# Both ends of a self-attention stage: feature loads cut into quarters, the first keys rotated earlier, softmax scalings moved to ScalarE, transposed-weight moves moved from ScalarE's queue to GpSimd's

## The chip, the cores and the metric

The program runs on one core of a Trainium2 chip. The metric is the device time of one execution in microseconds (us). The execution before the change takes 3047.43 us, the median of three runs (3047.22 to 3047.49). A difference of less than about 0.2% (6 us) can't be told from no change.

## The reference, cut to what matters

One post-norm decoder layer, in float32, over 2048 tokens of width 512:

```
x = layernorm(x + self_attention(x))        # 32 heads of 128, 8 key/value heads, no mask
x = layernorm(x + cross_attention(x, ctx))  # 32 sequences of 64 tokens
x = layernorm(x + ffn(x))

# self-attention; k_sel, v_sel are 512 gathered cache rows, 64 new tokens are appended
q, k, v = x @ wq.T, x @ wk.T, x @ wv.T      # q and k rotated by cos, sin
k_full, v_full = concat(k_sel, k[0]), concat(v_sel, v[0])     # 576 keys
out = softmax(q k_full^T / sqrt(128)) v_full @ wo.T
```

Every query attends to the same 576 keys (512 cached, 64 new). The change touches self-attention alone, at its first few and its last four units of work.

## The kernel before, in words

**Units.** Self-attention is 128 units, `units[n] = (g, tb, h)`: 8 groups g of 4 heads, 4 token blocks tb of 512 tokens, 4 heads h of the group. The four units of one (g, tb) are called a block here, b = n // 4; there are 32 blocks. A unit has four tiles i of 128 queries.

**A tile** (`scores(n, i)`): TensorE (PE) writes 128x576 scores to one of two PSUM buffers `s` (L651). VectorE (DVE) takes the row maximum `nmax` (L656), ScalarE (ACT) computes the exponentials `p` and their sum `den` (L659), DVE takes the reciprocal (L668), scales `p` by it (L669) and transposes 32x32 blocks of `p` into `T` (L677; in the order of instructions, the transpose of a tile stands behind the maximum of the next tile, except for a unit's last tile).

**Moves.** When `T` of a unit is full, `move(n)` (L689) issues 16 DMAs of 64 or 80 KB, SBUF to SBUF, which finish the transpose into `pT`. They are issued by SyncE's queue (SP). For the units in `short` (0, 1, 2, 124, 125, 126) only 12 of the 16 go there; the last four (`ranges = (3,)`) are issued one unit later by ACT's queue (`move(n - 1, (3,), nc.scalar)`).

**Values.** Two units later, `values(n - 2)` and `shared_values` multiply `pT` with the gathered values (L697, tile `po`), and ACT copies the result to `oT` (L720).

**Between the tiles**, PE works on two other matrix products, each in seven steps of 8 matmul instructions (L312, a Strassen-Winograd scheme with sums of operands): the queries of the next block (`q_step`; PSUM tiles `q_..`) and the output projection of an earlier one (`w_step`; `w_..`). The sums of their operands are made by GpSimd (POOL): `token_sums` (`tx1` to `tx4`), `left_sums` (weights), `output_sums` (`so1` to `so4`), 1.27 us each. In the first unit the products are what is left of block 0's queries (`last_products`: 3, 7 and 4); in the last four units there are no queries left, so only two or so products a unit stand between the tiles.

**Loads.** `load_features` fetches 512 tokens of `xT` (1 MB) with one DMA at the end of a block, ahead of that unit's moves in SP's queue; block 2's is issued at unit 0. At unit 124 the same is done for the first encoder block `encT` (1 MB), and at the end of unit 123 the eight DMAs of cross-attention's first weights (`load_kv_left`, tile `xwkv`) are put ahead of that unit's moves.

**Queues and order.** The instruction order of PE, DVE and ACT is the one written by hand; SP's and POOL's order, behind the start, is chosen when the program is built. A DMA waits, before it is issued, for the DMA that stood eight places earlier in the count of all hardware-queue DMAs (SP's and ACT's together); POOL's DMAs have a count of their own, of eight as well. An instruction that waits holds what stands behind it on its engine.

**Start.** Before unit 0, keys of group 0 are gathered by POOL (`gather_keys`, four indirect DMAs, tile `kn`), rotated in two halves by DVE and POOL (`rotate`, L593 to L598, into `kr`), transposed by PE (L632, `startbank`), and copied to `kT` by ACT (L635). Meanwhile PE makes four of block 0's seven query products.

Of the kernel before, what the change touches and what calls it, by code (L numbers as in the profile page):

```python
# [9 lines left out]
F32 = mybir.dt.float32  # L10
I32 = mybir.dt.int32
AF = mybir.ActivationFunctionType
ALU = mybir.AluOpType
# [3 lines left out]
P = 128  # L17
DIM = 512
NH, NKV, HD = 32, 8, 128
REP = NH // NKV  # L20
NT = 2048
SEQ = 64
TB = 512
NTB = NT // TB
# [28 lines left out]
def decoder_layer(  # L53
# [52 lines left out]
    def token_room(b, name):  # L106
        return act.tile([P, NC, TB], F32, tag=f"xT{b % 2}", name=name)

    def load_features(dst, src, tb, queue=nc.sync):
        queue.dma_start(  # L110
            out=dst, in_=src[:, tb * TB : (tb + 1) * TB].rearrange("(c p) n -> p c n", p=P)
        )

    def rows(src, tb):
        return src[tb * TB : (tb + 1) * TB, :].rearrange("(p j) f -> p j f", p=P)
# [100 lines left out]
    def left_sums(eng, a11, a12, a21, a22, s):  # L216
        eng.tensor_tensor(s[3], a11, a21, ALU.subtract)
        eng.tensor_tensor(s[1], a21, a22, ALU.add)
        eng.tensor_tensor(s[2], s[1], a11, ALU.subtract)
        eng.tensor_tensor(s[4], a12, s[2], ALU.subtract)  # L220
# [245 lines left out]
              for g in range(NKV)]  # L466
    KV_ORDER = (1, 6, 5, 7, 2, 4, 3)

    def load_kv_left(gp, pre):

        w = operands(pre, f"xwkv{gp}")
        s21 = w[5]
        for dst, (k, m) in ((w[1], (0, 0)), (w[2], (1, 0)), (w[4], (1, 1)), (s21, (0, 1))):
            for i in range(2):
                c0 = (i * NKV + 2 * gp + m) * HD
                nc.sync.dma_start(
                    out=dst[:, :, i * HD : (i + 1) * HD],
                    in_=xwkv[k * HF : (k + 1) * HF, c0 : c0 + HD].rearrange(
                        "(c p) n -> p c n", p=P
                    ),  # L480
                )
        left_sums(nc.gpsimd, w[1], w[2], s21, w[4], {1: w[5], 2: w[6], 3: w[7], 4: w[3]})
        return w

    def keys_values(gp, tb, tiles, tags):
# [14 lines left out]
    with ExitStack() as ph:  # L500
# [143 lines left out]
        def scores(n, i):  # L644


            g, tb, h = units[n]
            u = f"{g}_{tb}_{h}_{i}"
            s = sc.tile([P, 2, 512], F32, tag="sc", name=f"s{u}")
            for a in range(2):  # L650
                nc.tensor.matmul(  # L651
                    s[:, a, :HALF], qTs[n // REP][:, units[n][2], i * P : (i + 1) * P],
                    kTs[g][:, a * HALF : (a + 1) * HALF], start=True, stop=True,
                )
            nmax = small.tile([P, 1], F32, tag="nmax", name=f"nmax{u}")
            nc.vector.tensor_reduce(nmax, s[:, :, :HALF], AX.XY, ALU.max, negate=True)  # L656
            p = sb.tile([P, NKEY], F32, tag="p", name=f"p{u}", bufs=4)
            den = small.tile([P, 1], F32, tag="den", name=f"den{u}")
            nc.scalar.activation(  # L659
                p.rearrange("q (a k) -> q a k", a=2), s[:, :, :HALF], AF.Exp,  # L660
                bias=nmax, accum_out=den,
            )
            if i == 0:
                Ts[n] = sb.tile([P, NBK, TPB, SQ], F32, tag="T", name=f"T{g}_{tb}_{h}")
                flush()
            else:
                turn(n, i - 1)
            nc.vector.reciprocal(den, den)  # L668
            nc.vector.tensor_scalar(p, p, den, None, ALU.mult)  # L669
            ps_[n, i] = p  # L670
            if i == TPB - 1:
                turn(n, i)
# [132 lines left out]
        nc.vector.tensor_tensor(wq0[5], wq0[5], wq0[4], ALU.add)  # L805
        nc.vector.tensor_tensor(t[2], q[1, 1], t[1], sub)
        nc.vector.tensor_tensor(wq0[6], wq0[5], wq0[1], sub)
        nc.vector.tensor_tensor(wq0[3], wq0[2], wq0[6], sub)
        nc.vector.tensor_tensor(nrm2, cs2, cs2, ALU.mult)
        nc.vector.tensor_tensor(sn2, sn2, sn2, ALU.mult)  # L810
        nc.vector.tensor_tensor(nrm2, nrm2, sn2, ALU.add)
# [10 lines left out]
        z = first.mul("z", 5, True)  # L822
        y = first.mul("y", 6, True)
        new_keys(0)
        rotate(0, 0, NKT // 2)
        nc.vector.tensor_tensor(c[1, 1], z, c[1, 0], ALU.add)
        nc.vector.tensor_tensor(c[0, 1], y, c[1, 0], ALU.add)
        rotate(0, NKT // 2, NKT)
        for j in range(NKT):
            gather_values(0, j)  # L830
        cached_keys(0, "s0")
        nc.vector.tensor_tensor(t[3], q[1, 1], q[0, 1], sub)
        nc.vector.tensor_tensor(t[4], q[1, 0], t[2], sub)
        tok[1] = token_sums(xTs[1], "tx1", nc.gpsimd)
        wo_cur[0] = load_right(woT[columns(0), :], "wo0", nc.gpsimd, first=wo_cur[0])

        def last_products(i):
            if i == 3:
                first.mul("z", 3)
                reads.append(lambda: nc.vector.tensor_tensor(c[0, 1], z, c[0, 1], ALU.add))  # L840
            elif i == 7:
                first.mul("y", 7)
                reads.append(lambda: nc.vector.tensor_tensor(c[1, 1], y, c[1, 1], ALU.add))
            else:
                first.mul("y", 4)
                reads.append(lambda: nc.vector.tensor_tensor(c[1, 0], y, c[1, 0], ALU.add))
# [15 lines left out]
        for n in range(N):  # L862
            b, h = divmod(n, REP)
            g, r = units[n][0], n % PER
            if r == REP and g + 1 < NKV:
                load_group(g + 1)
            if r in gathers and g + 1 < NKV:
                gather_keys(g + 1, gathers[r])
            if 0 < n <= PER:


                b2, j = divmod(n - 1, TPB)
                nc.scalar.dma_start(out=acc[b2][:, j, :], in_=rows(x, b2)[:, j, :])
            if r == 2 * REP and g + 1 < NKV:
                later.append(lambda g=g: new_keys(g + 1))
            if r == 2 * REP + 1 and g + 1 < NKV:
                rotate(g + 1)
                later.append(lambda g=g: cached_keys(g + 1))
            if n == N - REP:
                encT[0] = big.tile([P, NC, TB], F32, tag="qT", name="encT0", bufs=2)  # L880
                load_features(encT[0], encT_in, 0)
            steps = {0: "qwqw", 1: "qw q", 2: "wqwq", 3: "w qw"}[h]

            def step(place):
                if n < REP:

                    i = {(0, 0): 3, (0, 1): 7, (0, 3): 4}.get((n, place))
                    if i:
                        last_products(i)
                    elif (n, place) in ((0, 2), (1, 0), (1, 1), (1, 2), (1, 3), (2, 0), (2, 2)):  # L890
                        q_step(n)
                elif steps[place] == "q":
                    q_step(n)
                elif steps[place] == "w":
                    w_step(b - 2 if h < 2 else b - 1)
                flush()

            def spare_bank():

                if n % 2 == 0 and later:  # L900
                    later.pop(0)()

            scores(n, 0)
            step(0)
            spare_bank()
            scores(n, 1)
            if n - 1 in short:
                move(n - 1, (3,), nc.scalar)
            if n >= 2:
                values(n - 2, 0, 2 if n % 2 == 0 else 3)  # L910
            step(1)
            scores(n, 2)
            step(2)
            if r in gathers and g + 1 < NKV:
                gather_values(g + 1, gathers[r])
            scores(n, 3)
            if n >= 2:
                values(n - 2, 2 if n % 2 == 0 else 3, NKT)
                if n % 2:
                    shared_values(n - 2)  # L920
            step(3)
            spare_bank()
            if h == REP - 1:
                if b + 2 < NB:
                    g2, tb2, _ = units[(b + 2) * REP]
                    if tb2 == 0:
                        wq_cur[g2] = load_left(wqT[:, columns(g2)], f"wq{g2}", nc.gpsimd)
                    tok[b + 2] = token_sums(xTs.pop(b + 2), f"tx{g2}_{tb2}", nc.gpsimd)
                elif b + 2 == NB:
                    kvw[0] = load_kv_left(0, "wq")  # L930
                else:
                    encR[0] = token_sums(encT[0], "te0", nc.gpsimd)
            if h == REP - 1 and b + 3 < NB or n == 0:

                b2 = b + 3 if n else 2
                xTs[b2] = token_room(b2, f"xT{b2}")
                load_features(xTs[b2], xT_in, b2 % NTB)
            move(n, (0, 1, 2) if n in short else range(NQD))

        encT[1] = big.tile([P, NC, TB], F32, tag="qT", name="encT1", bufs=2)
        load_features(encT[1], encT_in, 1)
        room = sb.tile([P, NBK, TPB, SQ], F32, tag="T", name="kvroom")
        room = room.rearrange("p b t k -> p (b t k)")
        tiles = [
# [504 lines left out]
```

## Time and profile before

| | |
|---|---|
| median of three runs | 3047.43 us |
| the profiled execution, its own time | 3049.76 us |
| its span in the profile | 3048.0 us |
| granted TensorE clock, mean | 0.997 |
| busy: PE / DVE / ACT / POOL | 3014.4 / 2200.1 / 783.8 / 946.9 us |
| self-attention, roughly | 18 to 1840 us of the span |
| idle PE, whole span (span less busy) | 33.6 us |

A row of the timeline starts with the start and the length in us of a run of like instructions; `x8` is their number, and the bracket at the end gives the idle time of the engine before the first of them and what ended it. PE executes matmuls one behind another and their ends are modelled, so a row of PE that is longer than others of the same kind and count also hides a loss. `SPq`, `ACTq` are DMAs issued by SP's and ACT's queue. Stretches can be asked for one by one, with the granted clock of each.

### The profile page before, as it was taken

How to read it: one execution, taken by the hardware profiler on the slowest of the kernel's cores; microseconds unless marked ns; L12 is line 12 of the kernel's file. 1: busy time of each engine (PE TensorE's matmuls, PEld its weight loads, DVE VectorE, ACT ScalarE, POOL GpSimd, SP SyncE). 2: the span in 40 equal slices, each digit the busy share in tenths (PEclk: the TensorE clock that was granted, in tenths of full speed). 3: DMA queues.
4: the chain of work that ended last, by engine and by line, in shares of the span. 5: the costliest groups of instructions: out<-in, count | busy, mean ns of one | idle time of the engine just before them, and what ended most of it. 6: DMA issues, size and time to landing. Idle time of an engine off the chain costs nothing.

```text
span 3048.0 us, 42453 instructions
## 1 busy us (share of the span) xinstructions
PE 3014.4 (99%) x14848; PEld 2321.9 (76%) x14848; DVE 2200.1 (72%) x4069; ACT 783.8 (26%) x1892; POOL 946.9 (31%) x774
## 2 busy tenths in 40 slices
PE   8999999999999999999999999999999999999998
PEld 6677777777777777777777768998888888888875
DVE  7777787777777777777877763546666666666787
ACT  2323223223222222222332221111111111111233
POOL 4231321321321321321321223035544444444420
PEclk9999999999999999999999999999999999999999
DMA  5444444444444444444444354351121121121121
GB/s 171 129 130 129 110 115 126 109 113 126 108 114 129 105 121 124 108 123 119 106 126 108 87 133 141 115 160 56 49 63 56 49 65 55 50 67 52 52 61 42
DMA packets 214931, 304.97 MB, mean 100 GB/s; under 512 B 45888, under 2 KB 108864, under 8 KB 214720
## 3 DMA queue, kind: packets, MB, share of 16 engines
q1 hardware_dynamic: 200048, 286.90, 34.7%
q10 hardware_dynamic: 12624, 11.16, 1.3%
q0 software_dynamic: 2048, 4.20, 0.5%
q8 instruction: 120, 1.97, 0.3%
q14 instruction: 91, 0.75, 0.1%
HBM read 107.05 MB, written 20.97 MB: 42 GB/s over the span
## 4 chain that ended last, share of the span: by engine, by line
PE 94%; DVE 2%; SPq 1%; DMA 1%; issue 1%; ACT 1%; POOL 0%; ACTq 0%; DVEq 0%; POOLq 0%
PE po L697 16%; PE s L651 15%; PE sx L1091 2%; PE pox L1163 2%; PE w_2y L312 1%; PE q_3y L312 1%; PE w_0y L312 1%; PE w_3y L312 1%; PE q_2y L312 1%; PE qx_0y L312 1%; PE wx_0y L312 1%; PE wx_3y L312 1%; PE qx_2y L312 1%; PE qx_1y L312 1%; PE wx_1y L312 1%; PE w_1y L312 1%
## 5 line engine op out<-in xcount | busy, mean ns | idle before, releaser
L659 ACT ACTIVATE p<-s,nmax 128x576 f32<-128x576 f32 x512 | 379.1, 740 | 1250.0 <-DVE nmax L656 1233.2
L651 PE MATMUL s<-kT,qT 128*128 128x288 f32 x2048 | 578.0, 408 | 4.9 <-ACT p L659 4.2
L697 PE MATMUL po<-pT,v 128*128 128x512 f32 (+1 forms) x1280 | 552.7, 605 | 6.2 <-DMA pT<-T 4.5
L651 PEld LDWEIGHTS s<-kT,qT 128*128 128x128 f32 x2048 | 388.4, 191 | 108.2 <-issue 19.7
L656 DVE TENSOR_REDUCE nmax<-s 128x1 f32<-128x576 f32 x512 | 384.0, 750 | 62.9 <-PE s L651 62.9
L677 DVE STREAM_TRANSPOSE T<-p 128x576 f32<-128x576 f32 x512 | 394.1, 770 | 4.4
L697 PEld LDWEIGHTS po<-pT,v 128*128 128x128 f32 (+1 forms) x1280 | 214.4, 190 | 208.5 <-issue 182.3
L669 DVE TENSOR_SCALAR p<-p,den 128x576 f32<-128x576 f32 x512 | 316.1, 617 | 17.9
L668 DVE RECIPROCAL den<-den 128x1 f32<-128x1 f32 x512 | 83.9, 164 | 230.9 <-ACT p L659 221.3
L283 POOL TENSOR_TENSOR so<-oT,oT 128x512 f32<-128x512 f32 x32 | 40.7, 1272 | 551.2 <-ACT oT L720 533.9
L286 POOL TENSOR_TENSOR so<-oT 128x512 f32<-128x512 f32 x32 | 40.6, 1270 | 351.2 <-ACT oT L720 100.6
L283 POOL TENSOR_TENSOR sox<-oTx,oTx 128x512 f32<-128x512 f32 x32 | 40.5, 1266 | 296.8 <-ACT oTx L1182 216.0
L1182 ACT ACTIVATE oTx<-pox,bv 128x128 f32<-128x128 f32 x256 | 73.7, 486 | 117.6 <-PE pox L1163 117.6
L224 POOL TENSOR_TENSOR tx<-xT 128x512 f32<-128x512 f32 x31 | 39.6, 1278 | 206.2 <-PE q_3z L312 65.0
L659 ACT ACTIVATION_READ_ACCUMULATOR p<-s,nmax 128x1 f32 x512 | 98.7, 193 | 0.0
L1292 POOL TENSOR_TENSOR txx<-x1T 128x512 f32<-128x512 f32 x31 | 39.3, 1268 | 174.6 <-PE qx_3z L312 75.2
L1108 ACT ACTIVATE ex<-ex 128x512 f32<-128x512 f32 x64 | 40.4, 631 | 201.7 <-DVE ex L1107 201.7
L1184 DVE TENSOR_SCALAR oTx<-pox,bv 128x128 f32<-128x128 f32 x256 | 72.6, 422 | 8.5 <-PE pox L1163 8.5
L1091 PEld LDWEIGHTS sx<-kvx,qTx 128*64 128x64 f32 x2048 | 62.3, 138 | 10.6 <-issue 10.6
L720 ACT COPY oT<-po 128x512 f32<-128x512 f32 x128 | 68.3, 587 | 4.7 <-PE po L697 3.8
L1091 PE MATMUL sx<-kvx,qTx 128*64 128x64 f32 x2048 | 66.7, 224 | 0.0
L1163 PE MATMUL pox<-pTx,kvx 64*128 64x256 f32 x512 | 64.6, 389 | 0.7 <-DMA pTx<-Tx 0.7
(443 smaller groups left out, 5746.1 us busy)
## 6 DMA issues: line engine op xcount, KB each, us to landing
pT<-T SPq DMA_DIRECT2D x1016, 80.0 KB
pT<-T SPq DMA_DIRECT2D x1008, 64.0 KB
xT<-in_xT SPq DMA_DIRECT2D x31, 1024.0 KB
kvx<-kv SPq DMA_DIRECT2D x32, 512.0 KB
pTx<-Tx SPq DMA_DIRECT2D x256, 64.0 KB
kv<-c SPq DMA_DIRECT2D x30, 512.0 KB
wo<-in_woT SPq DMA_DIRECT2D x32, 256.0 KB
xwq<-in_xwq SPq DMA_DIRECT2D x32, 256.0 KB
```

The costliest lines, as they stand in the source:

```text
L283: nc.gpsimd.tensor_tensor(t[1], a[1, 0], a[1, 1], ALU.add)
L312: nc.tensor.matmul(self.banks[b][:, m, :], self.left[i][:, k, m * P : (m + 1) * P], self.right[i][:, k, :], start=(first and m + k == 0), ...
L651: nc.tensor.matmul(s[:, a, :HALF], qTs[n // REP][:, units[n][2], i * P : (i + 1) * P], kTs[g][:, a * HALF : (a + 1) * HALF], start=True, s ...
L656: nc.vector.tensor_reduce(nmax, s[:, :, :HALF], AX.XY, ALU.max, negate=True)
L659: nc.scalar.activation(p.rearrange("q (a k) -> q a k", a=2), s[:, :, :HALF], AF.Exp, bias=nmax, accum_out=den,)
L668: nc.vector.reciprocal(den, den)
L669: nc.vector.tensor_scalar(p, p, den, None, ALU.mult)
L677: nc.vector.transpose(Ts[n][:, :, i, :], ps_.pop((n, i)).rearrange("q (b k) -> q b k", k=SQ))
L697: nc.tensor.matmul(pos[n].rearrange("d (a q) -> d a q", a=NQD), vs[units[n][0]][rows, v, :], pTs[n // 2][rows, :, chunk, :], skip_group_ch ...
L1091: nc.tensor.matmul(s[b * SEQ : (b + 1) * SEQ, i * REP + h, :], qTs[n][:, h, pr * HF + c0 : pr * HF + c0 + SEQ], kvs[n][:, pr, 0, c0 : c0 + ...
L1163: nc.tensor.matmul(po[pr, b][:, i, :].rearrange("d (h a j) -> d h a j", h=REP, a=2), kvs[n][r, pr, 1, i * HD : (i + 1) * HD], pTs[n][r, :, ...
L1182: nc.scalar.activation(dst, src, AF.Identity, bias=bias)
```

## The change

- `load_pieces` loads a feature block in four DMAs of 256 KB (one of the four groups of 128 features each). The pieces of block b + 2 are issued two by two in the first and second unit of block b (second and third unit for b = 0), in place of one 1 MB load at the end of block b - 1. The first encoder block's four pieces are spread over units 124 to 127 and the eight weight loads `xwkv` over units 124 to 126 (three, three, two), each ahead of the moves of its unit; the second encoder block comes in four pieces as well.
- The two halves of `rotate(0, ...)` come earlier in DVE's order, among the sums of the first weights, and product 3 of block 0's queries is put ahead of the first scores. One product less follows the fourth tile of unit 0 or 1.
- In units 0 to 3 all tiles, and in units 124 to 127 the tiles 1 and 3, are scaled by ACT (`activation(p, p, AF.Copy, scale=den)`) and not by DVE.
- The four moves of the `short` units that ACT's queue issued are issued by POOL's.

```diff
+    def load_pieces(dst, src, tb, *cs):
+        for c in cs:
+            nc.sync.dma_start(
+                out=dst[:, c, :], in_=src[c * P : (c + 1) * P, tb * TB : (tb + 1) * TB]
+            )
...
-    def load_kv_left(gp, pre):
+    def kv_left_parts(gp, pre):
...
-                nc.sync.dma_start(
+                loads.append(lambda dst=dst, k=k, i=i, c0=c0: nc.sync.dma_start(
...
+        return w, loads, lambda: left_sums(
+            nc.gpsimd, w[1], w[2], s21, w[4], {1: w[5], 2: w[6], 3: w[7], 4: w[3]}
+        )
...
             nc.vector.reciprocal(den, den)
-            nc.vector.tensor_scalar(p, p, den, None, ALU.mult)
+            if n < REP or n >= N - REP and i % 2:
+                nc.scalar.activation(p, p, AF.Copy, scale=den)
+            else:
+                nc.vector.tensor_scalar(p, p, den, None, ALU.mult)
...
         nc.vector.tensor_tensor(wq0[6], wq0[5], wq0[1], sub)
+        rotate(0, 0, NKT // 2)
         nc.vector.tensor_tensor(wq0[3], wq0[2], wq0[6], sub)
+        rotate(0, NKT // 2, NKT)
...
         new_keys(0)
-        rotate(0, 0, NKT // 2)
         nc.vector.tensor_tensor(c[1, 1], z, c[1, 0], ALU.add)
         nc.vector.tensor_tensor(c[0, 1], y, c[1, 0], ALU.add)
-        rotate(0, NKT // 2, NKT)
+        nc.vector.tensor_tensor(t[3], q[1, 1], q[0, 1], sub)
         for j in range(NKT):
             gather_values(0, j)
         cached_keys(0, "s0")
-        nc.vector.tensor_tensor(t[3], q[1, 1], q[0, 1], sub)
+        first.mul("z", 3)
         nc.vector.tensor_tensor(t[4], q[1, 0], t[2], sub)
+        nc.vector.tensor_tensor(c[0, 1], z, c[0, 1], ALU.add)
...
-            if n == N - REP:
-                encT[0] = big.tile([P, NC, TB], F32, tag="qT", name="encT0", bufs=2)
-                load_features(encT[0], encT_in, 0)
+            b2, k = b + 2, h - (b == 0)
+            if b2 < NB and k in (0, 1):
+                if k == 0:
+                    xTs[b2] = token_room(b2, f"xT{b2}")
+                load_pieces(xTs[b2], xT_in, b2 % NTB, 2 * k, 2 * k + 1)
+            if n >= N - REP:
+                if n == N - REP:
+                    encT[0] = big.tile([P, NC, TB], F32, tag="qT", name="encT0", bufs=2)
+                    kvw[0], kv_loads, kv_sums = kv_left_parts(0, "wq")
+                load_pieces(encT[0], encT_in, 0, h)
+                for load in kv_loads[3 * h : 3 * h + 3]:
+                    load()
+                if n == N - 2:
+                    kv_sums()
...
-                    i = {(0, 0): 3, (0, 1): 7, (0, 3): 4}.get((n, place))
+                    i = {(0, 0): 7, (0, 2): 4}.get((n, place))
                     if i:
                         last_products(i)
-                    elif (n, place) in ((0, 2), (1, 0), (1, 1), (1, 2), (1, 3), (2, 0), (2, 2)):
+                    elif (n, place) in ((0, 1), (0, 3), (1, 0), (1, 1), (1, 2), (2, 0), (2, 2)):
                         q_step(n)
...
             if n - 1 in short:
-                move(n - 1, (3,), nc.scalar)
+                move(n - 1, (3,), nc.gpsimd)
...
-                elif b + 2 == NB:
-                    kvw[0] = load_kv_left(0, "wq")
-                else:
+                elif b + 2 > NB:
                     encR[0] = token_sums(encT[0], "te0", nc.gpsimd)
-            if h == REP - 1 and b + 3 < NB or n == 0:
-                b2 = b + 3 if n else 2
-                xTs[b2] = token_room(b2, f"xT{b2}")
-                load_features(xTs[b2], xT_in, b2 % NTB)
             move(n, (0, 1, 2) if n in short else range(NQD))
...
         encT[1] = big.tile([P, NC, TB], F32, tag="qT", name="encT1", bufs=2)
-        load_features(encT[1], encT_in, 1)
+        load_pieces(encT[1], encT_in, 1, *range(NC))
```

## The prediction

> **What bounds the kernel now.** I read the page's busy table first, then PE's waits, then PE's timeline at both ends of self-attention, and last the queues and engines named there. PE is busy for 3014.4 of 3048.0 us, so little can be had, and all of it lies where PE waits or runs slowly. From 200 to 1760 us PE's waits sum to 1.3 us; the change's places are the first four and the last four units. There PE's timeline reads:
>
> ```profile
> 45.33 1.88 PE L697 MATMUL po<-pT,v 128*128 128x512 f32 x4
> 47.85 1.24 PE L651 MATMUL s<-kT,qT 128*128 128x288 f32 x4 [0.64 <-ACT p L659]
> ...
> 55.55 1.24 PE L651 MATMUL s<-kT,qT 128*128 128x288 f32 x4 [1.81 <-ACT p L659]
> 58.49 2.29 PE L651 MATMUL s<-kT,qT 128*128 128x288 f32 x4 [1.70 <-ACT p L659]
> 60.58 4.46 PE L697 MATMUL po<-pT,v 128*128 128x512 f32 x6
> ...
> 1776.74 2.81 PE L697 MATMUL po<-pT,v 128*128 128x512 f32 x6 [1.20 <-issue]
> ...
> 1792.12 3.75 PE L697 MATMUL po<-pT,v 128*128 128x512 f32 x4 [3.11 <-DMA pT<-T]
> ```
>
> See the brackets, and then the lengths: four score matmuls take 1.24 us at 55.55 and 2.29 behind the next gap; four `po` take 1.88 at 45.33 and 3.75 behind the gap at 1792. The stretches say why, in the column behind the busy times (granted clock):
>
> ```profile
> 58.00:62.00 4.00, 3.50 (x6) 2.19 (x7) 2.67 (x7) 1.27 (x4) 0.00 (x0) 0.50 0.38 110
> 66.00:80.00 14.00, 14.00 (x53) 9.05 (x52) 11.69 (x23) 6.60 (x15) 3.26 (x3) 1.00 0.61 166
> 1794.00:1798.00 4.00, 4.00 (x8) 2.29 (x7) 0.86 (x3) 0.04 (x1) 0.00 (x0) 0.50 0.73 185
> ```
>
> So both ends pay the gap and about 4 us at half clock after it. What the gaps wait for is on ACT and SP:
>
> ```profile
> 53.32 1.24 ACTq L689 DMA_DIRECT2D pT<-T  x2
> 54.67 0.74 ACT L659 ACTIVATE p<-s,nmax 128x576 f32<-128x576 f32 x1 [3.94 <-DVE T L677]
> ```
> ```profile
> 44.60 0.37 SPq L110 DMA_DIRECT2D xT<-in_xT  x1
> 45.65 44.88 SPq L689 DMA_DIRECT2D pT<-T  x53
> ```
> ```profile
> 1760.31 4.47 SPq L476 DMA_DIRECT2D xwkv<-in_xwkv  x8
> 1764.88 10.02 SPq L689 DMA_DIRECT2D pT<-T  x16
> 1775.01 0.52 SPq L110 DMA_DIRECT2D encT<-in_encT  x1
> 1775.88 35.94 SPq L689 DMA_DIRECT2D pT<-T  x36
> ```
>
> ACT's exponentials stand behind its own queue's moves, which wait for the DMA eight places earlier; at 45.65 that is held up by the 1 MB load issued at 44.60 (the chain of waits has "45.65 7.65 DMA pT<-T"). At the end, 8 weight loads and 1 MB stand in front of the moves that PE waits for at 1792. The third limit is the serial loop of a tile, in the chain of waits:
>
> ```profile
> 39.53 0.68 DVE nmax L656
> ...
> 40.29 0.84 ACT p L659 x2
> ...
> 41.15 0.17 DVE den L668
> ...
> 41.35 0.52 DVE p L669
> 41.87 0.60 DVE qT L364
> 42.47 0.68 DVE nmax L656
> ```
>
> It turns once in 2.94 us; PE's tile with one product is 0.97 + 1.73 = 2.70 (chain rows "PE s L651 x4", "PE q_2x L312 x8").
>
> **The change, part by part: the start.** From the end of the key transposes (18.93) to unit 4's first scores (68.83) 49.9 us pass. PE's work in it, at full clock: 16 scores x 0.97 = 15.5, 10 products x 1.73 = 17.3, `po` 3.44 + 2.57 + 1.92 = 7.9; sum 40.7. So 9.2 us are lost. None of this work is removed; only its order and the waits change.
> - Product 3 ahead of the first scores: it fills the 0.75 us that the first scores waited for ACT's key copy. Its DVE read (0.6) delays the first maximum, within the 1.5 us DVE was idle before it. The rotation moved up (eight DVE operations, about 2.2 us; POOL's four with it) doesn't start PE earlier: the transposes at 18.26 follow 17.30 + 1.0 us of PE work without a gap. 0 to 1.0 us, taken at 0.75.
> - ACT's scaling has no row. Nearest is ACT's exponential of 128x512 in SBUF in cross-attention (631 ns), scaled by size 0.7 us; from above the row of `p` itself, 0.74. In the loop it runs beside DVE's next maximum (0.68), so the loop falls from 2.94 to 0.17 + 0.6 + 0.68 + 0.84 + 0.1 = 2.4, below PE's 2.70; in unit 3 without products 1.8 against PE's 2.1. At a unit's last tile it costs 0.2 more than DVE's 0.52, since the transpose waits for it. DVE's own rows stretched by POOL (1.32 at 25.67, 1.58 at 50.96 for L669) go as well. ACT holds 0.84 + 0.7 + at most 0.6 of copies per tile: under 2.7.
> - The four moves leave ACT, so the 3.94 us wait goes. On POOL no direct DMA has a row; nearest are the gathers of as many 512-byte rows:
>
> ```profile
> L559 POOL DMA_INDIRECT v<-in_v_cache,row x32: 940/944/1483, 18.3 to 1483.5; - x32
> ...
> DMA to landing us min/median/max: 2.5/2.9/5.7
> ```
>
>   With 0.3 us between issues (73.79 after 72.53) a move costs POOL 1.25 us, four 5.0, and lands 2.9 later (from above 6.6, the median of the `kn` gathers; below, SP's 2.0). What queues behind them: POOL's `wo` sums end at about 35.7 (five us earlier sums follow PE's earlier products), unit 0's four run to 40.7 and land by 43.6; PE needs them at 44.2. `tx_2` sums behind them are due from 66. Unit 1's run 44.8 to 49.8, landed 52.7, due 53.3; unit 2's 54 to 59, due 63.
> - The load of block 2 in quarters and block 3's 1 MB out of unit 0's end: SP's first move of unit 1 goes at 44.1 with nothing large in front. Twelve at 0.64 (16 in 10.02) end at 51.8 and land 2.0 later, 53.8, against 53.3: 0.5 us of wait stays.
>
> Walking PE, DVE and ACT through units 0 to 3 with these rows leaves about 0.6 us of loop at unit 3, 0.5 of moves and 0.3 of boundaries: 9.2 - 1.4 = 7.8 us won.
>
> **The end.** From 1773.43 (scores of unit 125) to 1814.23 (values of unit 126) 40.8 us pass; the same rows sum to 32.7, so 8.1 are lost. Now unit 123's 16 moves go first, at 1762.6, and land by 1775 (wait of 1.20 gone). One encoder quarter and three weights (0.5 each) follow, and unit 124's twelve moves run 1775 to 1782.7, landed 1784.7; PE gets to them at 1787.2: the 3.11 and the slow clock behind it go. POOL issues unit 125's four between three `so` sums: 4 x 1.25 + 3 x 1.35 = 9.1 from 1786.4, last one landed 1797.2, due 1798.5; `so2` is ready at 1791.6, due 1795.8. The `xwkv` and `te` sums end at about 1811, due 1815. Half the scalings stay on DVE: there the loop is still 2.3, and two accumulations (0.6, 1.21) stand in it, so 1.5 us remain at units 126 and 127, and 0.5 for unit 126's moves. 8.1 - 2.0 = 6.1 us won.
>
> **The middle.** 31 blocks get three DMAs more each on SP (1.5 us of 0.5 each) beside 64 moves x 0.64 = 41 us in a block of 56: hidden; the load is due a whole block later than its issue. POOL's `so2`, `so4` now stand ahead of `tx3`, which is 2.6 us later, with `tx1` after it as before: hidden. Two or three waits on `pT` and `wq` (0.64 at 197.78, 0.44 and 0.20 near 633 to 651) may shrink: 0.5.
>
> **Two rules of the Trainium skill against the trace.** "DMA: Bandwidth & Descriptors", section "Bandwidth", "Measured", says to batch DMAs to 1 MiB and more, since each has about 2.0 us fixed. By it, four quarters (2.6 each) take 10.4 us in place of 4.4; at the end, with two encoder blocks in quarters, 12 us would be against us. The trace: SP issues move behind move every 0.64 us while each takes 2 to land, so the fixed part overlaps; only 0.5 us of SP each counts, and there is room for it. I take the trace. "TensorE: Matmul & The Clock Gate", section "Part 1: The HAM clock gate", has the clock halve after an idle window of about 3.4 us. By it gaps of 1.81 and 1.70 with a burst between cost only themselves, and the start would give 2.0 us less (1.12 + 0.41 + 0.46 over the full-clock lengths). The rows above show half clock, so I count them; the same rows warn that a gap left at two or three us costs twice.
>
> **Sum.** 7.8 + 6.1 + 0.5 = 14.4 us. The span 3048.0 becomes 3033.6; the profiled execution's 3049.76 becomes 3035.4. That one is 2.3 above the median of the runs, so the median becomes 3047.4 - 14.4 = 3033.0. If all is won at both ends and in the middle: 9.2 + 8.1 + 1.3 = 18.6, 3029.
>
> **Rivals.**
> - *POOL's moves come late* (6.6 us to land): unit 0's wait 2 us, unit 125's 3, each with half clock behind it (2 to 3 us): some 7.5 us given back, 3040.5. For it: `kn`'s 6.6. Against: `v` gathers in the same stage, 2.9.
> - *SP stays the bound of the start*: 53 moves in 44.88 us is 0.85 each; at that pace unit 1's land at 56.3, 3 us late, and the clock drops: 5.5 back, 3038.5. Against: the 0.85 holds the wait for the 1 MB load.
> - *Slower: a direct move costs POOL far more than a gather.* It has a row per block of `T`, 128 or 160 runs. POOL is in order, so each us over the 1.6 that fits unit 0's and 1's slack is paid four times at five places, and beyond 2.3 us each the gaps pass 3 us and add 3 of slow clock. At 2.3 the gain is gone; at 3.0 it is 5 x (5.6 + 3) - 14.4 = 29 worse, and halving that for overlap, 3060. Against: the gathers' 0.94, never over 1.48.
> - *The waits go but PE waits as long later* (unit 5's moves on a full SP queue, or the accumulations before cross-attention): 3046.
>
> **How the numbers follow.** Both ends won 0.72; POOL late 0.11, SP bound 0.09, slower 0.06, nothing 0.02. The likeliest gives 3033.0, with its own bounds 3029 to 3037. The range 3028.5 to 3041.5 takes in the SP case and most of POOL's. A measurement can tell 0.2% (6.1 us) from no change; so faster is below 3041.3: 0.72 + 0.08 + 0.06 = 0.86; same 0.08; slower 0.06.
>
> **What would show it.** Right: no PE gap over 1 us and clock 1.0 from 19 to 1850; unit 4's scores near 61 and values of unit 126 near 1800 (8 and 6 earlier, together); ACT never behind a DMA; POOL's moves near 1.25 us apart. Wrong: `po` waiting for `pT` near 44, 53 or 1790 with half clock after it, or POOL's moves over 2 us apart.

## The result, and the profile after

The changed kernel takes 3037.33 us (median of nine runs, 3034.30 to 3041.03); the kernel before beside it took 3047.33 (nine, 3045.55 to 3049.19). The ratio is 0.997, 95% interval 0.9961 to 0.9978: about 10 us faster. Forecast were 14.4 us and 3033.0 us.

The profiled execution of the changed kernel took 3034.3 us, span 3032.2; the one of before 3049.76 and 3048.0. From span to span it is 15.8 us, from median to median 10.0. That difference turned out to be the lesson of this case. (The changed kernel's profiled execution was the fastest of its nine.)

PE's timeline of the changed kernel at the same places (start, length, run of instructions, idle time before it in brackets; line numbers are those of the changed file: L667 scores, L718 values, L710 moves, L675 exponentials, L688 ACT's scaling):

```profile
52.71 2.81 PE L718 MATMUL po<-pT,v 128*128 128x512 f32 x6 [0.50 <-issue]
...
59.31 1.24 PE L667 MATMUL s<-kT,qT 128*128 128x288 f32 x4
...
64.61 1.96 PE L718 MATMUL po<-pT,v 128*128 128x512 f32 x4 [1.36 <-DMA wv<-in_wvT]
...
1777.40 1.88 PE L718 MATMUL po<-pT,v 128*128 128x512 f32 x4
...
1798.63 3.70 PE L718 MATMUL po<-pT,v 128*128 128x512 f32 x8 [0.41 <-ACT oT L741]
```

The gaps of 1.81 and 1.70 us are gone, and so is the 3.11 before unit 124's values (now at 1777.40, four `po` in 1.88). Unit 4's scores come at 59.31 (68.83 before), unit 126's values at 1798.63 (1814.23 before). A wait of 1.36 at 64.61 is new. Every row shown has its full-clock length, and the stretches say the same in the column of the granted clock (0.50, called half clock here, in 58 to 62 and 1794 to 1798 before):

```profile
60.00:66.00 6.00, 4.64 (x19) 3.08 (x18) 3.98 (x10) 3.87 (x8) 3.27 (x3) 1.00 0.86 222
...
1794.00:1798.00 4.00, 4.00 (x16) 2.10 (x14) 2.92 (x6) 2.32 (x6) 2.62 (x2) 1.00 0.44 113
```

POOL's and SP's timelines of the changed kernel, for the moves:

```profile
43.28 1.98 POOL L710 DMA_DIRECT2D pT<-T  x4 [2.96 <-DVE T L698]
```
```profile
52.69 19.53 SPq L710 DMA_DIRECT2D pT<-T  x28
...
1763.22 1.46 SPq L484 DMA_DIRECT2D xwkv<-in_xwkv  x3
1765.01 8.74 SPq L710 DMA_DIRECT2D pT<-T  x12
```

A direct move occupies POOL for 0.50 us (median of 24, landing 3.0 us later). SP issues one move per 0.70 us at 52.69 and still comes late for unit 2's values.

For the comparison of profiles, five marks were read from PE's timeline: a = the key transposes (`startbank`), b = unit 4's first scores, c = the first output product (`w_0x`), d = unit 126's first scores, e = unit 126's values. Times in us between them:

| kernel | a | a to b | b to c | c to d | d to e | a to e | e to end |
|---|---|---|---|---|---|---|---|
| before | 18.26 | 50.57 | 24.82 | 1691.42 | 29.16 | 1795.97 | 1233.77 |
| before, second profile | 18.61 | 48.01 | 25.67 | 1690.55 | 28.21 | 1792.44 | 1235.65 |
| after | 17.27 | 42.04 | 25.95 | 1688.37 | 25.00 | 1781.36 | 1233.57 |
| after, second profile | 17.44 | 42.02 | 26.12 | 1688.45 | 25.02 | 1781.61 | 1233.75 |
| moves on ACT | 18.68 | 45.48 | 28.75 | 1689.04 | 31.81 | 1795.08 | 1233.84 |
| scaling on DVE | 17.68 | 48.35 | 26.19 | 1688.82 | 26.21 | 1789.57 | 1233.55 |
| whole loads | 17.36 | 41.94 | 32.61 | 1690.20 | 25.15 | 1789.90 | 1233.64 |
| rotation back | 18.77 | 42.31 | 25.87 | 1688.16 | 25.03 | 1781.37 | 1235.46 |
| next group's weights later | 18.39 | 42.84 | 25.61 | 1689.01 | 25.01 | 1782.47 | 1233.74 |
| POOL's moves alone | 17.14 | 51.43 | 25.54 | 1690.43 | 26.28 | 1793.68 | 1233.98 |
| ACT's scaling alone | 18.53 | 49.04 | 25.89 | 1692.11 | 30.55 | 1797.59 | 1235.68 |
| pieces alone | 16.95 | 48.84 | 28.16 | 1688.93 | 27.44 | 1793.37 | 1233.78 |
| POOL issues more | 18.60 | 42.10 | 25.11 | 1687.72 | 25.02 | 1779.95 | 1233.75 |
| and unit 3's | 18.99 | 41.78 | 23.86 | 1688.48 | 25.01 | 1779.13 | 1233.58 |

In POOL's moves alone and pieces alone, a to b holds a wait of 0.99 and 0.62 us inside the key transposes themselves.

### The profile page after: what moved, and what is told of

Its sections match the earlier page's. It is cut to its first block, busy times and chain, and to the rows that moved or that the text cites. A ratio compares the mean times of both kernels' runs of the same rounds, so it can differ in the third digit from the quotient of the medians.

```text
span 3032.2 us, 42610 instructions
## 1 busy us (share of the span) xinstructions
PE 3005.9 (99%) x14848; PEld 2318.4 (76%) x14848; DVE 2187.9 (72%) x4045; ACT 801.7 (26%) x1916; POOL 961.5 (32%) x798
## 4 chain that ended last, share of the span: by engine, by line
PE 96%; DVE 2%; DMA 1%; POOL 0%; ACT 0%; issue 0%; ACTq 0%; DVEq 0%; POOLq 0%
PE po L718 16%; PE s L667 16%; PE sx L1119 2%; PE pox L1191 2%; PE w_1y L318 1%; PE q_3y L318 1%; PE w_0y L318 1%; PE w_3y L318 1%; PE q_1y L318 1%; PE q_0y L318 1%; PE qx_0y L318 1%; PE wx_0y L318 1%; PE qx_3y L318 1%; PE wx_3y L318 1%; PE wx_1y L318 1%; PE q_2y L318 1%
## 5 line engine op out<-in xcount | busy, mean ns | idle before, releaser
L675 ACT ACTIVATE p<-s,nmax 128x576 f32<-128x576 f32 x512 | 379.1, 740 | 1211.3 <-DVE nmax L672 1166.6
L667 PE MATMUL s<-kT,qT 128*128 128x288 f32 x2048 | 575.3, 407 | 0.5 <-ACT p L675 0.5
L718 PE MATMUL po<-pT,v 128*128 128x512 f32 (+1 forms) x1280 | 549.1, 602 | 2.5 <-DMA wv<-in_wvT 1.4
L667 PEld LDWEIGHTS s<-kT,qT 128*128 128x128 f32 x2048 | 387.7, 190 | 101.6 <-issue 19.7
L718 PEld LDWEIGHTS po<-pT,v 128*128 128x128 f32 (+1 forms) x1280 | 213.3, 189 | 202.5 <-issue 175.3
L690 DVE TENSOR_SCALAR p<-p,den 128x576 f32<-128x576 f32 x488 | 305.3, 626 | 17.1
L675 ACT ACTIVATION_READ_ACCUMULATOR p<-s,nmax 128x1 f32 x512 | 98.7, 193 | 0.0
```

The lines of the kernel that those rows point to most:

```text
L667: nc.tensor.matmul(s[:, a, :HALF], qTs[n // REP][:, units[n][2], i * P : (i + 1) * P], kTs[g][:, a * HALF : (a + 1) * HALF], start=True, s ...
L675: nc.scalar.activation(p.rearrange("q (a k) -> q a k", a=2), s[:, :, :HALF], AF.Exp, bias=nmax, accum_out=den,)
L718: nc.tensor.matmul(pos[n].rearrange("d (a q) -> d a q", a=NQD), vs[units[n][0]][rows, v, :], pTs[n // 2][rows, :, chunk, :], skip_group_ch ...
```

## The experiments

Medians below stand beside the median of the kernel before in the same series (3046.3 to 3046.7 us).

**The changed kernel again.** No edit.

> The changed kernel again, unaltered, to have its time on the same chip as the three that follow and a second profile of it. Theory A (the gain is the waits and the half clock at both ends, and nearly all of it is won in every run): ratio to the kernel before 0.9965 to 0.9972, 8.5 to 10.5 us, and the profile again shows clock 1.00 in 20:60 and 1760:1800 us. Theory B (the gain hangs on waits near 1 us that tip into half clock in some runs): the profile shows half clock behind some wait on a moved block (the candidate is unit 2's values near 64.6 us, which waited 1.36 us for a weight load), and its time is 3 or more us over the first profile's 3034.3. Theory C (what differs is before 13 us, where the first products run slower in one profile than in another): the later stretches agree and only the first products' lengths differ, by 1.7 us or so.

Measured: 3036.78 us (before 3046.70), ratio 0.997 (0.9959 to 0.9981): 9.9 us faster. The new profile agrees with the first in a to e within 0.25 us, and the clock is 1.00 in every stretch read, from 5 us on. Theory A holds for the ends in this profile, and nothing of B shows in it. But B isn't excluded for the other runs: the two profiled executions are the fastest of their nine and seven, the sixteen runs reach from 3034.30 to 3041.03, and five of them, all at 3037.68 or above, have a mean granted clock of 0.998 against 0.999 in the profiled two. Where those lose time is open. Some of what differs between runs lies outside: over all profiles a falls between 16.95 and 18.99 and the rest behind e between 1233.6 and 1235.7, whatever the kernel. Theory C named the first of the two.

**Moves back on ACT.**

```diff
-                move(n - 1, (3,), nc.gpsimd)
+                move(n - 1, (3,), nc.scalar)
```

> The changed kernel with one part undone: the last four blocks' moves of a short unit are issued by ACT again and not by POOL. Theory A (each part takes away its own wait): ACT's exponential stands behind moves that wait for an earlier transfer, as it did for 3.94 us near 54 us; two gaps of 1.8 and 1.7 us and about 2 us of half clock come back at the start, and perhaps 1 us at the end: 4 to 6 us slower than the changed kernel. Rival (ACT's wait was only the shadow of the 1 MB load on the other queue, and the quarters took that away): ACT issues its moves without a wait over 1 us, and it is 0 to 1.5 us slower, ratio to the kernel before within 0.001 of the changed kernel's.

Measured: 3050.06 us (before 3046.70), ratio 1.0008 (1.0002 to 1.0015): 13.3 slower than the changed kernel, and slower than before. Both expectations were far too small. ACT's timeline of this kernel, then PE's:

```profile
49.42 2.87 ACTq L710 DMA_DIRECT2D pT<-T  x4
52.33 0.74 ACT L675 ACTIVATE p<-s,nmax 128x576 f32<-128x576 f32 x1 [2.14 <-DMA pT<-T]
```
```profile
82.05 4.27 PE L718 MATMUL po<-pT,v 128*128 128x512 f32 x6 [3.19 <-DMA pT<-T]
```

Issuing four moves takes ACT's queue 2.5 to 3.4 us (0.6 each and what they wait), and ACT now has 0.74 + 0.19 + 0.78 us of work per tile. So the exponential behind a short unit's moves comes some 2 us late (2.14 us above), the units behind it too, and unit 3's values wait 3.19 us with half clock after it. Half of the loss is at the other end: d to e takes 31.81 us against 25.00. There PE waits 1.64 us for an accumulation, 1.36 us for an exponential and 3.37 us for ACT's copy of an earlier result, at full clock:

```profile
1813.76 3.70 PE L718 MATMUL po<-pT,v 128*128 128x512 f32 x8 [3.37 <-ACT oT L741]
```

ACT's queue does not have room for the moves and the scalings.

**Scaling back on DVE.**

```diff
-            if n < REP or n >= N - REP and i % 2:
+            if False:
```

> The changed kernel with one part undone: all scalings by the reciprocal stay with DVE. Theory A (the serial loop of a tile was the third limit): the loop is again 2.9 us against PE's 2.7, so PE waits some 0.2 us on the exponentials at each of about ten tiles, and more in unit 3 and at the end: 3 to 5 us slower than the changed kernel, by short waits, without half clock. Rival (the loop only showed because ACT and the transfers were late): PE's waits on the exponentials stay at 0.5 to 1 us in all and it is within 1 us of the changed kernel.

Measured: 3042.48 us (before 3046.70), ratio 0.9986 (0.9980 to 0.9993): 5.7 slower than the changed kernel. Theory A in place and nearly in size, but not without half clock. PE in unit 3, where no product stands between the tiles:

```profile
53.79 1.24 PE L667 MATMUL s<-kT,qT 128*128 128x288 f32 x4 [0.45 <-ACT p L675]
56.73 2.08 PE L667 MATMUL s<-kT,qT 128*128 128x288 f32 x4 [1.70 <-ACT p L675]
```

The distance 2.94 is the loop of the prediction, 1.70 what is left of it behind four score matmuls of 1.24. So the 1.70 of before, which the prediction read as ACT standing behind its moves, is the loop's: here ACT has no moves and it is the same. With ACT's scaling, two exponentials at the same place of the changed kernel follow each other in 1.75 us:

```profile
53.34 0.74 ACT L675 ACTIVATE p<-s,nmax 128x576 f32<-128x576 f32 x1 [1.49 <-DVE nmax L672]
...
55.09 0.73 ACT L675 ACTIVATE p<-s,nmax 128x576 f32<-128x576 f32 x1
```

**Whole loads.** Edit: all feature blocks from block 2 on, the two encoder blocks and the eight `xwkv` loads at their old places, by `load_features` and `load_kv_left` as in the kernel before.

> The changed kernel with one part undone: block 2's features, the two encoder blocks and the eight weight loads at the end are loaded whole, at the places where the kernel before has them. Theory A (the queue of moves behind 1 MB is what PE waited for): unit 1's values near 53 us and unit 124's near 1790 us wait again for a moved block, 3 us each with half clock behind them, and ACT no longer suffers since it has no moves: 6 to 10 us slower than the changed kernel, most of the gain. Rival (with the four moves on POOL and the loop shorter, the load is covered): 0 to 3 us slower.

Measured: 3043.94 us (before 3046.70), ratio 0.9992 (0.9984 to 1.0): 7.2 slower than the changed kernel. Theory A in size; the places are others than it named: unit 2's values, not unit 1's, and unit 123's, not unit 124's. PE's timeline, then SP's:

```profile
69.62 3.75 PE L718 MATMUL po<-pT,v 128*128 128x512 f32 x4 [6.38 <-DMA pT<-T]
```
```profile
50.81 0.52 SPq L110 DMA_DIRECT2D xT<-in_xT  x1
52.78 37.33 SPq L710 DMA_DIRECT2D pT<-T  x43
```

SP issues the moves behind the 1 MB load at 0.87 us each, and unit 2's values wait 6.38 us, half clock behind. At the end, d to e is 25.15 against 25.00, and 1.57 us are lost earlier, before unit 123's values. The 3.11 before unit 124's values, laid to the loads ahead of the moves, does not come back. The edit undoes the size of the loads and their places together; no run separates the two.

**Rotation back.** Edit: `rotate` behind the products, product 3 among unit 0's tiles, the steps of `q_step` as before.

> The changed kernel with one part undone: the keys are rotated after the products, the first group's product 3 is multiplied among the first tiles and not ahead of the scores, and that group's later products take the steps they had before. Theory A (this part brings only what PE waited for ACT's key copy, taken at 0.75 us): 0.5 to 1.5 us slower than the changed kernel. Rival (the one product more among the first tiles sits where DVE and ACT have no slack, so the units after it come late as with the other parts): 4 or more us slower, with waits for moved blocks behind unit 0.

Measured: 3036.66 us (before 3046.53), ratio 0.9968 (0.9956 to 0.9980): the changed kernel's time. Neither expectation came true. Its profile has the 0.75 us wait for ACT's key copy, and gains it back: from mark a, unit 0's values come at 26.75 us (25.74 in the changed kernel), unit 1's at 35.79 (35.44), unit 2's at 47.49 (47.34). PE arrives later at blocks that are late, and waits less: 0 in place of 0.50 before unit 1's.

**The next group's weights later.**

```diff
-            if r == REP and g + 1 < NKV:
+            if r == REP + 2 and g + 1 < NKV:
                 load_group(g + 1)
```

> The changed kernel, and the next group's cached weights (two loads of 256 KB and what follows) are loaded two units later. Theory A (unit 2's values at 64.6 us wait 1.36 us because these loads stand in the transfer engines ahead of the moves): that wait goes, unit 3's of 0.24 too, and nothing else is late, since the group is needed tens of us on: 1.3 to 2 us faster than the changed kernel, ratio to the kernel before near 0.9963. Rival (the moves themselves are issued too late, at one per 0.70 us, and the loads only share the time): the wait stays over 0.8 us and the time is that of the changed kernel within 0.7 us. Second rival: the loads collide two units later, with the gathers or with unit 4's moves, and it is no faster or up to 2 us slower.

Measured: 3036.72 us (before 3046.53), ratio 0.9966 (0.9952 to 0.9980): no gain. Theory A falls, and the first rival (the moves are issued too late) holds:

```profile
66.22 1.96 PE L718 MATMUL po<-pT,v 128*128 128x512 f32 x4 [1.06 <-DMA pT<-T]
```

With the two loads out of the way unit 2's values still wait 1.06 us (1.36), now put down to the moves themselves, and 0.44 us is lost two units later. The releaser "DMA wv" of the first profile was, by this, only the transfer that landed last beside them.

**POOL's moves alone** (the kernel before and this one part).

```diff
-                move(n - 1, (3,), nc.scalar)
+                move(n - 1, (3,), nc.gpsimd)
```

> The kernel before with one part alone: the last four blocks' moves of a short unit are issued by POOL. Theory A (parts in a row: with ACT free the next limit is the loads in front of SP's moves and the loop on DVE): ACT's 3.94 us wait is gone, but unit 1's or 2's values wait for a block instead: 1 to 5 us faster than the kernel before. Rival 1 (POOL's moves are nearly the whole change, as undoing them costs more than the whole gain): 8 to 10 us faster. Rival 2 (the parts only pay together): within 1 us of the kernel before.

Measured: 3045.99 us (before 3046.53), ratio 0.9998 (0.9990 to 1.0007): no difference, Rival 2. The loop takes the place of ACT's wait: PE's timeline has the 1.70 again, and half clock.

```profile
59.29 2.29 PE L651 MATMUL s<-kT,qT 128*128 128x288 f32 x4 [1.70 <-ACT p L659]
```

**ACT's scaling alone** (the kernel before and this one part: the four lines of the diff at `reciprocal`).

> The kernel before with one part alone: ACT does the scalings of the first four units and of half the tiles of the last four. Theory A (ACT's queue has no room for both: four moves take it 2.5 to 2.9 us of issue and a scaling 0.78, so each exponential behind them is later than before): slower than the kernel before by 1 to 5 us, with waits of PE on the exponentials at every short unit's end. Rival (the shorter loop pays by itself, as undoing it costs 5 us): 1 to 4 us faster than the kernel before.

Measured: 3052.55 us (before 3046.53), ratio 1.0019 (1.0011 to 1.0027): 6.0 slower, Theory A (expected up to 5). ACT's timeline:

```profile
49.85 3.95 ACTq L692 DMA_DIRECT2D pT<-T  x4
53.85 0.74 ACT L659 ACTIVATE p<-s,nmax 128x576 f32<-128x576 f32 x1 [3.22 <-DMA pT<-T]
```

**Pieces alone** (the kernel before and this one part).

> The kernel before with one part alone: the loads in pieces, spread among the moves, with the four moves on ACT and all scalings on DVE. Theory A (the parts only pay together, the more so as the pieces give PE's blocks early while ACT still waits for its own moves): within 1.5 us of the kernel before. Theory B (parts in a row, each its own): 4 to 7 us faster, as undoing it in the changed kernel cost 7.

Measured: 3045.56 us (before 3046.69), ratio 0.9997 (0.9989 to 1.0005): no difference that can be told, Theory A.

So the parts alone give -0.5, +6.0 and -1.1 us, and all together -9.9. Of the pairs (rotation, worth nothing, left in): POOL's moves with pieces -4.2, POOL's moves with scaling -2.8, pieces with scaling +3.4. The gain is one of all three at once.

**The kernel before again**, one execution. (The mark that the expectation calls unit 125's scores is d, unit 126's.)

> The kernel before, unaltered, for a second profile of it: the prediction's sum was made on a profile that lies 2 to 3 us above the median of this kernel, the two profiles of the changed kernel lie 2 to 3 us below theirs. From the first scores the stages of the first profile are 49.17 us to unit 4's scores, 24.82 to the first output product, 1691.42 to unit 125's scores, 29.16 to unit 126's values. Theory A (the losses at the ends are the same in every run, and what differs lies before 20 us and after 1830 us): the same four within 0.3 us. Theory B (the waits and the half clock behind them differ from run to run in this kernel, and the first profile was a bad one): one of the four is 1.5 to 4 us shorter.

Measured: Theory B. Its time was 3048.52 us, on one run. All four stages differ, by 0.85 us or more (b to c is the longer one here; from the first scores to unit 4's 46.43 us against 49.17), and from the key transposes to unit 126's values it needs 3.5 us less than the first profile. PE's timeline:

```profile
57.74 1.24 PE L651 MATMUL s<-kT,qT 128*128 128x288 f32 x4 [1.71 <-ACT p L659]
58.81 2.74 PE L697 MATMUL po<-pT,v 128*128 128x512 f32 x6
```

The gap is the one of the first profile (1.70), the rows behind it have the full-clock lengths (2.29 and 4.46 there). The 1.81 ahead of it is 0.53 here. The time is still 1.8 us above the median of this kernel: what the second profile saves between a and e it gives back in part behind e (1235.65 against 1233.77).

**POOL issues more.** SP's 0.70 us per move was left as the cause of the wait at 64.61, so POOL, idle from 55 to 62 us, takes eight of the 16 moves of units 1 and 2.

```diff
-                move(n - 1, (3,), nc.gpsimd)
+                move(n - 1, (2, 3) if n in (2, 3) else (3,), nc.gpsimd)
...
-            move(n, (0, 1, 2) if n in short else range(NQD))
+            move(n, (0, 1) if n in (1, 2) else (0, 1, 2) if n in short else range(NQD))
```

> The changed kernel, and POOL also issues the third block's moves of units 1 and 2, so SP has eight of each to issue in place of twelve. POOL had nothing to do there from 55 to 62 us. Theory A (SP's pace of 0.70 us for a move is what makes unit 1's values wait 0.5 and unit 2's 1.36 us): both waits go, nothing takes their place, 1.5 to 2 us faster than the changed kernel, ratio to the kernel before near 0.9962. Rival (the transfers behind the issue are at their limit, and a move takes longer to land when more are under way): the waits stay over half of what they are, within 0.8 us of the changed kernel.

Measured: 3034.07 us (before 3046.69), ratio 0.9961 (0.9947 to 0.9974). Theory A: both waits are gone, a to e is 1779.95, 1.4 to 1.7 less than in the changed kernel's two profiles. The gain over the kernel before is 12.6 us against 9.9, but the intervals of the two ratios overlap. Something did take the place of the waits in part: the wait at unit 3's values, whose 16 moves SP still issues alone, grows from 0.24 to 0.97.

```profile
76.38 2.84 PE L718 MATMUL po<-pT,v 128*128 128x512 f32 x6 [0.97 <-DMA pT<-T]
```

**And unit 3's.** As above with `(2, 3) if n in (2, 3, 4)` on POOL, `(0, 1) if n in (1, 2, 3)` on SP, and the condition in front widened to `n - 1 in short or n == REP`, so that unit 3's are issued there too.

> As the run before, and POOL also issues the third and fourth block's moves of unit 3, which SP issued all sixteen. In the run before, unit 3's values waited 0.97 us for a moved block at 76 us. Theory A (SP's pace again): that wait goes; POOL's eight moves put the two gathers at 63 us some 4 us later, which nothing waits for: 0.5 to 1 us faster than the run before, some 3.5 faster than the changed kernel, first scores to unit 126's values near 1776.6 us. Rival (the blocks are late because more transfers are under way, not because they are issued late): the wait stays or moves to the next unit, same time as the run before within 0.5 us.

Measured: 3033.29 us (3031.52 to 3033.43; before 3046.33), ratio 0.9955 (0.9942 to 0.9969). Theory A for the wait: no wait for a block is left at either end, unit 3's values run at 75.31 without one, and b to c falls from 25.11 to 23.86. From c to d 0.76 us are given back, and the time, 0.4 us better than the run before when each is taken from its own kernel before, is what the rival allowed too. Each of its five runs is below each of the changed kernel's sixteen (3034.30 at least), though in another series; the intervals of the two ratios overlap.

## Why the prediction was right, and where it was not

- **On its own profile the sum came out**: 14.4 forecast, and from a to e the first profile of before and the first of after differ by 14.6 (1795.97 - 1781.36). The start won 8.5 (a to b), forecast 7.8, and gave 1.1 back behind it (b to c: the 1.36 us of unit 2's values, which the walk had not seen; it took unit 2's moves to be in time for 63). The end won 5.6 (from 1773.43 and 1763.44, unit 125's scores, to unit 126's values), forecast 6.1; the middle 1.6, forecast 0.5. That the sum is met so closely is in part luck: the parts are off by up to 1.1 us, and the errors cancel. In the middle PE's waits sum to 1.3 us from 90 to 1773 us before (the prediction's 1.3 "from 200" holds the 0.64 at 197.78) and to 0.1 after.
- **The step that failed is the last one**, "that one is 2.3 above the median of the runs, so the median becomes 3047.4 - 14.4". The excess of that execution was taken for something that the change leaves alone. The second profile shows otherwise: between a and e, where the change acts, it needs 3.5 us less (1792.44 against 1795.97), and outside 2.2 us more (18.61 + 1235.65 against 18.26 + 1233.77). So the excess of 2.3 hid a larger one at the mended places. With 2.3 taken off the gain, 3047.4 - 12.1 = 3035.3 would have been forecast; with 3.5, 3036.5; measured were 3037.33. The 11 us between the second profile of before and the changed kernel's two (1792.44 against 1781.36 and 1781.61) stand near the 10 of the medians. How the other runs of either kernel divide isn't shown, since two profiles of each are kept.
- **The signs.** Unit 4's scores near 61 and unit 126's values near 1800 came (59.31, 1798.63). "No PE gap over 1 us" did not: the 1.36 stands. Nor did POOL's moves 1.25 us apart.
- **ACT behind its own moves**: right as a wait, mis-sized as the cause. Of the two gaps at 55 to 58 us only the first is ACT's; the 1.70 is the loop of unit 3 and stays when ACT is free (POOL's moves alone, scaling on DVE). The prediction had the loop as its third limit, but put its 2.94 beside a PE tile of 2.70, not beside unit 3's bare 1.24.
- **POOL's moves**: forecast 1.25 us each, 0.50 measured. The gather was the wrong neighbour for the issue, the right one for the landing (2.9 forecast, 3.0 measured). The rival "slower" needed 2.3 us a move to cancel the gain.
- **SP**: forecast 0.64 per move, 0.70 measured. The 0.5 us left at unit 1's values came as forecast; unit 2's 1.36 is the same shortage one unit later, as the runs with POOL's help show. So the rival "SP stays the bound of the start" was right in kind: waits of 0.50 and 1.36 us without half clock, where it had 3 us with it. That its 3038.5 lies nearer to the measured median than 3033.0 doesn't bear its sum out: it gave 5.5 us back for half clock that isn't there.
- **ACT's scaling**: 0.7 forecast, 0.78 measured. **The loop** without products: 1.8 forecast, 1.75 measured.
- **Product 3 and the rotation**: 0.75 us forecast, no difference that can be told. The term was counted as won, though the next step of the same walk left waits for moved blocks behind it.
- **The end**: "8 weight loads and 1 MB stand in front of the moves that PE waits for at 1792" was not the cause. With the loads whole and POOL's moves that wait is gone, also in POOL's moves alone; with the pieces and ACT's moves it is 0.47 us, with ACT's scaling alone 0.58. The trace of before shows what held the moves: from 1775.88 to 1783.57 SP issued one move and then stood idle for 7.2 us, put down to a move and not to a load. The chain of waits has the move that ACT issued at 1780.10, and then SP; both use the same semaphore of the common eight:

```profile
1780.10 3.45 DMA pT<-T
...
1783.57 0.51 SPq L689
```

  So in this kernel ACT's moves held the end, too, by way of SP's queue. What remains with the pieces alone is the loop and ACT (2.18 us for an exponential).
- **The two rules.** Against the Trainium skill's "DMA: Bandwidth & Descriptors", section "Measured" (batch to 1 MiB), the trace's reading held: undoing the pieces, size and places together, cost 7.2 us. (The 2.0 us, and with it the prediction's estimates of 2.6, 4.4, 10.4 and 12 us, come from that page's section "Anatomy of one DMA — SWDGE (gpsimd) path", which is on DMAs that GpSimd issues; these loads are SP's.) For "TensorE: Matmul & The Clock Gate", Part 1, the choice to count half clock was right for the profile at hand and too firm in general; see the last section. What the rule would take off the start is some 2.8 us by the rows, not 2.0: from row to row four scores take 2.09 us against 0.97, six `po` 4.30 against 2.57.

## What to carry to other kernels

An excess of one profiled execution over the median is not a constant to be carried along: ask which stage it sits in, and if it may be the stage under change, take it off the gain, or take a second profile. Parts that serve one loop (who scales, who issues, what stands ahead in the queue) are limits in a ring: freeing one shows the next, undoing one of three cost 6 to 13 us where all three gain 10, and the sum of single effects (+4.4) had the wrong sign. Before work is moved to an engine, count what else its instruction queue issues: four moves of 0.6 us each were more than ACT could carry beside the scalings, and POOL issued them in 0.5 each while it was idle.

## What was not expected of the hardware

The same gaps do not always cost the same clock. A gap of 1.70 or 1.71 us in front of unit 3's second tile had half clock behind it in four profiles (before, POOL's moves alone, scaling on DVE, pieces alone) and none in the second profile of before. The gap ahead of it does not part them: 0.45 us in three of the four, 0.53 in the one without. Single gaps: 2.37 us with half clock behind (pieces alone, `po` in 4.51), 2.09 without (scaling on DVE, at 82.82, 2.81), 3.37 without (moves on ACT, at 1813.76, eight `po` in 3.70, shown above).

```profile
82.86 4.51 PE L718 MATMUL po<-pT,v 128*128 128x512 f32 x6 [2.37 <-DMA pT<-T]
```
```profile
82.82 2.81 PE L718 MATMUL po<-pT,v 128*128 128x512 f32 x6 [2.09 <-DMA pT<-T]
```

The Trainium skill's page "TensorE: Matmul & The Clock Gate", Part 1, says that the activity window runs freely and does not start with the kernel, which would make the cost of a gap a matter of where it falls. The runs fit that, but none of them shows the window. They do not fit the 3.4 us that the page gives for an idle window as a bound on the gap: 2.37 sufficed. For a forecast, a gap near 2 us at this density of work is a chance of 1.6 to 2.8 us more (what the rows behind these gaps are longer by), not a certain cost. Such chances make up most of the 3.5 us between the two profiles of before: its start lost some 2.8 us in the slow rows of one profile and none in the other. The changed kernel, without these gaps, repeats from a to e within 0.25 us in its two profiles; its whole times over nine runs, 3034.30 to 3041.03, vary no less than the nine of before, 3045.55 to 3049.19, and no profile shows where.
